# Routing of the first half of the tokens moved behind layer 2, two of its sums split, and a norm's bias kept with the rows

## The chip, the core and the metric

The kernel runs on one core of a Trainium2 chip. A core has a matrix engine (TensorE, PE in the profile), three engines for elementwise work (VectorE or DVE, ScalarE or ACT, GpSimd or POOL), a queue engine (SyncE, SP), an on-chip memory of 128 partitions, accumulators (PSUM) that the matrix engine writes, and 16 DMA engines. The metric is the time of one execution on the device in microseconds (us); lower is better.

## The reference

One layer of a graph network with a mixture of experts, on 1250 tokens of 768 numbers in float32:

```python
xn = layernorm(x)
x = x + gnn(xn, edges) + performer(xn)      # two attention layers over the graph, linear attention
x = x + experts(layernorm(x))

# gnn: layer 1 has 4 heads of 192, layer 2 has 2 heads of 96
out2 = gat(gat(layer_norm(xn), 4 heads), 2 heads)
gnn = concat([xn, out2]) @ Wu + bu

# experts: 8 experts, each token goes to its best 2
probs = softmax(flat @ router_w.T)
top, idx = top_k(probs, 2)
weights = top / balance[idx], normalised to sum 1  # balance: from the sum of probs over all tokens
h = silu(flat @ w1[e].T); y = h @ w2[e].T
out = sum over the token's two experts of weight * y
```

The edges are 20,000 drawn ones and a loop on every token.

## The kernel before

**Tiles.** The tokens are ten tiles of 125 rows. Tiles 0 to 4 are the first half, 5 to 9 the other half. The residual rows x live on chip in `acc[:, t, :]`; a row there is DX = 770 numbers wide: 768 values, and behind them two columns for the row's mean and the reciprocal of its deviation (rstd).

**Up to layer 2.** The program builds the adjacency counts, runs layer 1 and the performer attention, and puts the part of the sum that is known without layer 2 into `acc` (`updates`, line 886).

**Layer 2.** `second_layer(h, half)` (line 933) computes head h of layer 2 for one half of the destination tokens. It has ten steps, one for each tile of source tokens. A step (`attend`, lines 816 to 826) is a chain: ScalarE makes two exponentials (L816, L818, both named `e_b`), VectorE takes the larger of the two (L820), caps it at 1 and multiplies by the edge counts (L822, `p_b`), and five matmuls add that into five PSUM tiles (L826, `pa_b`). After ten steps the sums are divided by their denominators (L945, L946) into `o2s`, called `o_5` to `o_9` for the other half.

The first half's two heads run first. The other half's two heads follow, 20 steps in all, and the first half's further work is drawn in between them through the generator `first_half` (line 1180), one piece for each step until it is used up. That work is, for each tile:

- `out_turned` (L950): the layer-2 output is transposed (`tr_o`, L150) and copied by ScalarE (`oT`, L955)
- `updated` (L960): eight matmuls with the layer-2 rows of Wu (L966) give 768 sums in one PSUM tile of two banks, VectorE adds them to the row (L971), and takes the row's statistics (L129, L130)
- `stored` (L993), once for a half: rstd of its rows, mean and rstd put beside the rows (L997, L998), and the rows written to DRAM on SP's queue, for the first half to two places, `x2_d` and `xh_d`
- `update_turned` (L976): the row is transposed (`tr_xm`) and copied (`xT`, L980)
- `logits` (L985): six small matmuls with the router's weights

Then the routing of the first half, nearly all of it on VectorE and in one go: `placed(…, 0, …)` (line 1097) ranks the eight logits of each token (L1114 to L1119), counts each expert's tokens by two matmuls (`pcum`, L1122 and L1123) and prefix sums (L1085), and finds each choice's position; `rows_of(0)` (L1146) writes one-hot rows for those positions.

In these steps the order on each engine is chosen by a list scheduler from the program's order and dependences.

**From there on the order is written by hand** for TensorE, VectorE, ScalarE and GpSimd: each runs its instructions in the order of the program. A loop over `i` from 0 to 7 takes the other half's five tiles through the same stages, one stage later for each i: `out_turned` of tile 5+i, `update_turned` of tile 3+i, `updated` of tile 4+i, `logits` of tile 2+i. Within it, `first_tiles` (line 1152) builds for each of the eight experts the list of its first 125 tokens out of the first half: masks at i = 0, and at i = 1 ten matmuls (`plist`, L1173) and the indices (`take`, L1175). Right after it GpSimd starts eight gathers (L1218), one for each expert's first tile, out of `xh_d`. At its end come `normed` and `turned` for the first tiles.

**Experts.** An expert tile q is 125 gathered rows. `normed(q)` (L1224) normalises them: for q < 8 VectorE makes the bias, minus mean times rstd (`nb`, L1229), and ScalarE applies scale and bias (`xme`, L1230); for later tiles VectorE does it alone (L1232). Then the rows are transposed (`tr_xe`, L150; `xTe`, L1242), multiplied with w1 (`ph`, L1260), gated (`hw`, L1269 on ScalarE and L1270 on VectorE), transposed again (`tr_he`, `hT`) and multiplied with w2 (`po`, L1489). VectorE works on the other half's routing, and the lists of all later tiles, between the gates of the first eight tiles. The second weights (`ew2`, eight loads of 768 KB on SP) are loaded when the updates are done. Results go to DRAM, are gathered by halves (L1506), added (L1515) and stored (L1516).

Of the kernel before, what the change touches and what calls it, by code (L numbers as in the profile page):

```python
# [9 lines left out]
F32 = mybir.dt.float32  # L10
# [3 lines left out]
AF = mybir.ActivationFunctionType  # L14
ALU = mybir.AluOpType
# [4 lines left out]
D = 768  # L20
P = 125
NT = N // P
KD = D // 128
H1, C1 = 4, 192
H2, C2 = 2, 96
MH, HD, MF = 12, 64, 32
NE, FI = 8, 256


NQ = NE + (2 * (P * NT // 2 - P) + P * NT + NE * (P - 1)) // P  # L30
DX = D + 2
NQ1 = (2 * N + NE * P // 2) // P
BIG = 8192.0
assert NQ == 33
# [39 lines left out]
def kernel(  # L74
# [3 lines left out]
    nc = tc.nc  # L78
# [729 lines left out]
    TH_ = NT // 2  # L808
# [148 lines left out]
        transposed(psum, o2s[t], [(0, C2), (C2, C2)], keep_o2, f"o2{t}", bufs=bufs)  # L957
        oTs[t] = oT

    def updated(psum, t):  # L960

        oT = oTs.pop(t)
        po = psum.tile([P, 2, 512], F32, tag="po", name=f"po2_{t}", bufs=1)
        for hb in range(2):
            for j in range(H2):
                nc.tensor.matmul(  # L966
                    po[:, hb, :384], oT[:, j, :], wub[:, j, hb * 384 : (hb + 1) * 384],
                    start=(j == 0), stop=(j == H2 - 1),
                )
        xa = acc[:, t, :D].rearrange("p (a c) -> p a c", a=2)  # L970
        nc.vector.tensor_tensor(xa, po[:, :, :384], xa, ALU.add)  # L971
        stats_of(g2p, acc[:, t, :D], mv3[:, t, :], f"c{t}")

    x2Ts = {}
# [1 line left out]
    def update_turned(psum, t, bufs=None):  # L976
        xT = g2p.tile([128, KD, P], F32, tag="xT", name=f"xT_{t}", bufs=2)

        def keep_xm(b0, n, pt):
            nc.scalar.copy(xT[:, b0 : b0 + n, :], pt[:, :n, :])  # L980

        transposed(psum, acc[:, t, :D], BLOCKS, keep_xm, f"xm{t}", bufs=bufs)
        x2Ts[t] = xT

    def logits(pl, t):  # L985

        xT = x2Ts.pop(t)
        for k in range(KD):
            nc.tensor.matmul(pl, xT[:, k, :], rw[:, k, :], start=(k == 0), stop=(k == KD - 1))
# [3 lines left out]
    def stored(hf):  # L993

        t0, t1 = hf * TH_, (hf + 1) * TH_
        rs3 = rs3s[hf] = rstd_of(small, mv3, "c", t0, t1)
        nc.vector.tensor_copy(acc[:, t0:t1, D : D + 1], mv3[:, t0:t1, 0:1])  # L997
        nc.vector.tensor_copy(acc[:, t0:t1, D + 1 : DX], rs3.unsqueeze(2))  # L998
        for t in range(t0, t1):
            nc.sync.dma_start(out=x2_t[:, t, :], in_=acc[:, t, :DX])  # L1000
            if not hf:
                nc.sync.dma_start(out=xh_t[:, t, :], in_=acc[:, t, :DX])

# [92 lines left out]
    def placed(psum, hf, pl):  # L1096

        hs = slice(hf * TH_, (hf + 1) * TH_)
        three, big8 = [P, TH_, NE], [P, TH_, NE, NE]
        off = rtc.tile(three, F32, tag="off", name=f"off_{hf}")  # L1100
        nc.vector.tensor_tensor(
            off, mv3[:, hs, 0:1].to_broadcast(three), csum.unsqueeze(1).to_broadcast(three), ALU.mult
        )
        nc.vector.tensor_tensor(off, pl, off, ALU.subtract)
        nc.vector.tensor_tensor(lg[:, hs], off, rs3s[hf].unsqueeze(2).to_broadcast(three), ALU.mult)
        if hf:

            nc.vector.tensor_reduce(red[:, 0, :], lg, AX.X, ALU.max)
            nc.vector.tensor_tensor(prob, lg, red[:, 0, :].unsqueeze(2).to_broadcast([P, NT, NE]), ALU.subtract)
            nc.scalar.activation(prob, prob, AF.Exp)  # L1110
        cmp, eq = (big[:, 3010 + 320 * i : 3330 + 320 * i].rearrange("p (t a b) -> p t a b", t=TH_, a=NE) for i in range(2))
        others = lg[:, hs].unsqueeze(2).to_broadcast(big8)
        own = lg[:, hs].unsqueeze(3).to_broadcast(big8)
        nc.vector.tensor_tensor(eq, others, own, ALU.is_equal)  # L1114
        nc.vector.tensor_tensor(eq, eq, before.unsqueeze(1).to_broadcast(big8), ALU.mult)
        nc.vector.tensor_tensor(cmp, others, own, ALU.is_gt)
        nc.vector.tensor_tensor(cmp, cmp, eq, ALU.add)
        nc.vector.tensor_reduce(rank[:, hs], cmp, AX.X, ALU.add)
        nc.vector.tensor_scalar(sel[:, hs], rank[:, hs], 2.0, None, op0=ALU.is_lt)  # L1119
        yield  # L1120
        pcum = psum.tile([P, 2, TH_, NE], F32, tag="rt" if hf else "tr", name=f"pcum_{hf}", bufs=1)
        nc.tensor.matmul(pcum[:, 0], upper, sel[:, hs], start=True, stop=True)  # L1122
# [12 lines left out]
        picked(0, hs, pos[:, hs].unsqueeze(2).to_broadcast([P, TH_, 2, NE]), pick)  # L1135
        over2 = rtc.tile([P, TH_ * 2, NT - 1], F32, tag="over2", name=f"over2_{hf}")
        nc.vector.tensor_tensor(
            over2, at[:, 0, hs].rearrange("p t k -> p (t k)").unsqueeze(2).to_broadcast([P, TH_ * 2, NT - 1]),
            tens[:, 1:].unsqueeze(1).to_broadcast([P, TH_ * 2, NT - 1]), ALU.is_ge,
        )  # L1140
        nc.vector.tensor_reduce(nth[:, hs].rearrange("p t k -> p (t k)"), over2, AX.X, ALU.add)
        nc.vector.scalar_tensor_tensor(r_[:, hs], nth[:, hs], -float(P), at[:, 0, hs], op0=ALU.mult, op1=ALU.add)

    def rows_of(hf):
        hs = slice(hf * TH_, (hf + 1) * TH_)
        nc.vector.tensor_tensor(  # L1146
            oh_r[:, hf * NT : (hf + 1) * NT, :],
            r_[:, hs].rearrange("p t k -> p (t k)").unsqueeze(2).to_broadcast([P, NT, P]),
            col.unsqueeze(1).to_broadcast([P, NT, P]), ALU.is_equal,
        )  # L1150
# [28 lines left out]
    def first_half():  # L1179
        for t in range(TH_):  # L1180
            out_turned(ps_c, t)
            updated(ps_c, t)
            yield
        stored(0)
        for t in range(TH_):
            update_turned(ps_c, t)
            yield
            pl = ps_c.tile([P, NE], F32, tag="tr", name=f"plg_{t}")
            logits(pl, t)
            nc.scalar.copy(lraw[:, t, :], pl)  # L1190
        for _ in placed(ps_c, 0, lraw):
            pass
        rows_of(0)

    fh = first_half()
    for h in range(H2):
        for _ in second_layer(h, 1):
            next(fh, 0)
    for _ in fh:
        pass  # L1200
    closed(gap_, pa_, psc_)
# [22 lines left out]
    def normed(q):  # L1224
        xg = xgs[q]
        xm = exa.tile([P, D], F32, tag="xm", name=f"xme_{q}", bufs=1)
        if q < NE:
            nb = exa.tile([P, 1], F32, tag="nb", name=f"nb_{q}")
            nc.vector.scalar_tensor_tensor(nb, xg[:, D : D + 1], -1.0, xg[:, D + 1 : DX], op0=ALU.mult, op1=ALU.mult)  # L1229
            nc.scalar.activation(xm, xg[:, :D], AF.Identity, bias=nb, scale=xg[:, D + 1 : DX])  # L1230
        else:
            nc.vector.tensor_scalar(  # L1232
                xm, xg[:, :D], xg[:, D : D + 1], xg[:, D + 1 : DX], op0=ALU.subtract, op1=ALU.mult
            )
        xms[q] = xm

# [49 lines left out]
    manual_ = tc.manual_schedule(engines={ET.PE, ET.DVE, ET.Activation, ET.Pool})  # L1286
    manual_.__enter__()
    plg = ps_x.tile([P, TH_, NE], F32, tag="rt", name="plg")
    ft = first_tiles(ps_x)
    for i in range(TH_ + 3):  # L1290
        if i < TH_:
            out_turned(ps_x, TH_ + i, bufs=3)
        if i == 0:
            next(ft)
        if 2 <= i <= TH_ + 1:
            update_turned(ps_x, TH_ + i - 2, bufs=3)
        if i == TH_ + 1:
            stored(1)
        if 1 <= i <= TH_:
            updated(ps_x, TH_ + i - 1)  # L1300
        if i == 1:
            for _ in ft:
                pass
            for q in range(NE):
                gather(q)
        if i >= 3:
            logits(plg[:, i - 3, :], TH_ + i - 3)
        if i == TH_:
            normed(0)
# [212 lines left out]
    rt = routed()  # L1522
# [117 lines left out]
```

## Time and profile before

| | us |
|---|---|
| median of three runs | 1060.87 |
| lowest and highest | 1057.02, 1064.84 |
| the profiled execution | 1066.33 |
| its span in the profile | 1064.5 |
| TensorE busy | 972.1 |
| VectorE busy | 646.6 |
| ScalarE busy | 386.3 |
| GpSimd busy | 158.1 |

The profile is one execution on the chip. A row of the groups or of the timeline names the start or the busy time, the engine, the source line, the operation, the output and the inputs, the shape, and how many instructions it stands for; in brackets, how long the engine had been idle before and what released it. PEld is TensorE's weight load, which runs beside its matmuls. The granted clock is the share of full speed at which TensorE was allowed to run. "issue" is time in which the engine waited for nothing that the profile shows. Matmul ends are modelled, so a busy TensorE is not always one at its peak, and neighbouring rows can overlap slightly.

### The profile page before, as it was taken

What the parts mean: (1) busy time and instruction counts of PE and PEld (TensorE: products, weight loads), DVE (VectorE), ACT (ScalarE), POOL (GpSimd) and SP (SyncE); (2) the same over time, 40 slices, a digit from 0 to 9 for tenths busy, and PEclk for the clock granted to TensorE, in tenths of its full rate; (3) what the DMA queues carried; (4) which work ended last, traced back from release to release, by engine and by line L of the source; (5) the groups of instructions that cost most, each with busy time, mean ns of one, the idle gap of its engine ahead of it and who ended that gap; (6) DMA issues with size and microseconds to landing.
All of it is one profiled execution on the core that took longest, in us unless ns stands there. A gap on an engine that the chain in (4) does not pass through costs nothing. (4 is left out here: it accounts for less than half of the span.)

```text
span 1064.5 us, 12124 instructions
## 1 busy us (share of the span) xinstructions
PE 972.1 (91%) x4323; PEld 663.0 (62%) x4323; DVE 646.6 (61%) x1407; ACT 386.3 (36%) x662; POOL 158.1 (15%) x157
## 2 busy tenths in 40 slices
PE   6899999999979989999999899999998979987980
PEld 2775455546645557777776765566677667765750
DVE  7699556207457556667768849576587454453441
ACT  1653333310000075566555610065465254322320
POOL 1010000000000000000000202432100402275533
PEclk9999999999889999999999999999998889998995
DMA  8410000212321010000022422111163565455442
GB/s 209 138 40 24 15 22 13 104 74 77 117 91 59 15 57 17 24 24 23 2 83 115 133 69 99 64 45 53 59 203 113 132 215 177 134 174 152 127 124 85
DMA packets 55424, 93.19 MB, mean 88 GB/s; under 512 B 22704, under 2 KB 29040, under 8 KB 55354
## 3 DMA queue, kind: packets, MB, share of 16 engines
q1 hardware_dynamic: 30966, 73.63, 20.4%
q0 software_dynamic: 15904, 17.02, 5.9%
q10 hardware_dynamic: 8484, 1.65, 0.9%
q8 instruction: 39, 0.64, 0.3%
q14 instruction: 31, 0.25, 0.1%
HBM read 75.53 MB, written 27.04 MB: 96 GB/s over the span
## 5 line engine op out<-in xcount | busy, mean ns | idle before, releaser
L826 PE MATMUL pa_a<-acc,p_a 125*125 125x197 f32 x800 | 143.5, 335 | 5.8 <-DVE h L850 3.4
L826 PEld LDWEIGHTS pa_a<-acc,p_a 125*125 125x125 f32 x800 | 135.0, 189 | 22.0 <-issue 12.4
L695 PE MATMUL pg<-W,xnT 128*125 128x396 f32 x240 | 84.4, 516 | 6.2 <-DVE acc L698 6.2
L897 PE MATMUL po<-wu_sb,xnT 128*125 128x384 f32 x240 | 82.0, 490 | 5.1 <-ACT acc L901 3.9
L820 DVE SCALAR_TENSOR_TENSOR e_a<-e_a,e_a 125x625 f32<-125x625 f32 x80 | 67.2, 846 | 27.9 <-ACT e_a L816 14.3
L530 PE MATMUL pk_q<-xnT,wq_sb 128*128 128x375 f32 (+1 forms) x216 | 81.5, 516 | 2.5 <-PEq L744 1.7
L822 DVE SCALAR_TENSOR_TENSOR p_a<-e_a,cntT 125x625 f32<-125x625 f32 x80 | 64.4, 811 | 29.7 <-PE pa_a L826 27.2
L530 PE MATMUL pk_k<-xnT,wk_sb 128*128 128x375 f32 (+1 forms) x216 | 82.0, 515 | 0.0
L816 ACT ACTIVATE e_a<-rowt_a,s 125x625 f32<-125x625 f32 x80 | 64.7, 817 | 37.6 <-DVE p_a L822 34.0
L346 DVE TENSOR_SCALAR ohd<-iota,dst_f 125x125 bf16<-125x125 int16 (+1 forms) x170 | 51.6, 304 | 40.3 <-PE pe L353 40.3
L1489 PE MATMUL po<-ew,hT 128*125 (+1 forms) x192 | 70.6, 513 | 5.5 <-DVE hT L1280 5.0
L493 DVE CUSTOM_DVE_ANT_0 junk<-nmr,rows 125x1250 f32<-125x1250 bf16 x40 | 58.3, 1457 | 27.1 <-DMA rows<-sr_d 21.5
L695 PEld LDWEIGHTS pg<-W,xnT 128*125 128x125 f32 x240 | 46.9, 196 | 43.1 <-DVE acc L698 6.8
L818 ACT ACTIVATE e_a<-rowt_a,s1x 125x625 f32<-125x625 f32 x80 | 64.0, 814 | 21.5 <-DVE e_a L820 21.1
L1260 PE MATMUL ph<-ew,xTe 128*125 (+1 forms) x288 | 69.3, 392 | 0.0
L897 PEld LDWEIGHTS po<-wu_sb,xnT 128*125 128x125 f32 x240 | 43.6, 188 | 35.8 <-ACT acc L901 6.5
L1260 PEld LDWEIGHTS ph<-ew,xTe 128*125 128x125 f32 x288 | 55.6, 195 | 12.0
L530 PEld LDWEIGHTS pk_q<-xnT,wq_sb 128*128 128x128 f32 x216 | 39.8, 189 | 36.4 <-issue 17.2
L342 DVE TENSOR_SCALAR ohs<-iota,smod,wgt 125x313 bf16<-125x313 int16 x170 | 60.6, 356 | 0.0
L535 ACT ACTIVATE sT_q<-pk_q,kb 128x375 f32<-128x375 f32 (+1 forms) x18 | 10.8, 602 | 135.2 <-PE pk_q L530 135.2
L1489 PEld LDWEIGHTS po<-ew,hT 128*125 128x125 f32 x192 | 36.2, 196 | 29.4 <-issue 5.2
L826 PEld LDWEIGHTS pa_b<-h,p_b 125*125 125x125 f32 x400 | 49.0, 192 | 8.2 <-DVE p_b L822 2.3
(349 smaller groups left out, 1543.6 us busy)
## 6 DMA issues: line engine op xcount, KB each, us to landing
y_d<-y SPq DMA_DIRECT2D x23, 375.0 KB
ew<-in_w1T SPq DMA_DIRECT2D x8, 768.0 KB
ew<-in_w2T SPq DMA_DIRECT2D x8, 768.0 KB
nmr<-nm_d SPq DMA_DIRECT2D x20, 305.2 KB
rowt_a<-ab_d SPq DMA_DIRECT2D x8, 610.4 KB
x_d<-acc SPq DMA_DIRECT2D x10, 376.0 KB
acc<-in_x SPq DMA_DIRECT2D x10, 375.0 KB
xr<-in_x SPq DMA_DIRECT2D x10, 375.0 KB
```

The source lines that it names most:

```text
L342: nc.vector.tensor_scalar(oh_s[:, :TH], iota[:, :TH], smod[:, c : c + 1], wgt[:, c : c + 1], op0=ALU.is_equal, op1=ALU.mult)
L493: nc.vector.tensor_tensor_reduce(out=junk, in0=nm, in1=row, scale=1.0, scalar=-3.0e38, op0=ALU.add, op1=ALU.max, accum_out=mx_col)
L530: nc.tensor.matmul(pk[:, :w], w_sb[:, k, f * 128 : (f + 1) * 128], xnT[:, k, t0 * P : (t0 + n) * P], start=(k == 0), stop=(k == KD - 1),)
L695: nc.tensor.matmul(pg, xnT[:, k, t * P : (t + 1) * P], W12[:, k, cs], start=(k == 0), stop=(k == KD - 1))
L816: nc.scalar.activation(e1, rowt[:, 0, :], AF.Exp, bias=s[:, h, 0, u : u + 1])
L818: nc.scalar.activation(e2, rowt[:, 1, :], AF.Exp, bias=sx[:, h, u : u + 1])
L820: nc.vector.scalar_tensor_tensor(e1, e1, 1.0, e2, op0=ALU.min, op1=ALU.max)
L822: nc.vector.scalar_tensor_tensor(p, e1, 1.0, cntT[:, u, hf * HN : (hf + 1) * HN], op0=ALU.min, op1=ALU.mult)
L826: nc.tensor.matmul(pas[i][:, :cw], p[:, i * P : (i + 1) * P], hv, start=(u == 0), stop=(u == NT - 1))
L897: nc.tensor.matmul(po[:, hf, :384], xnT[:, k, ts], wu_sb[:, k, cs], start=(k == 0), stop=False)
L1260: nc.tensor.matmul(ph, xT[:, k, :], ew1[:, whose_r[q], k, :].rearrange("p o i -> p (o i)"), start=(k == 0), stop=(k == KD - 1),)
L1489: nc.tensor.matmul(po[:, hf, :384], hT[:, c, :], ew2[:, e_r, c, hf * 384 : (hf + 1) * 384].rearrange("p o n -> p (o n)"), start=(c == 0), ...
```

## The change

There are three edits.

**Where the first half's routing stands.** `first_half` now ends with the logits. Its pieces are no longer taken one a step from the first step on, but spread over the 20 steps of the two heads (at steps 1, 3, 4, 6, 8 and 9 of the first head, counted from 0, and 1, 3, 4, 6, 7 and 9 of the second; there are eleven pieces, so the last call finds nothing left), and a tile's logits are one piece behind its transposing. The ranks are placed in the hand-ordered loop at i = 0, the rest of `placed` at i = 1 after the update of tile 5, `rows_of` and the masks of `first_tiles` at i = 2 after the update of tile 6, and the lists with the eight gathers at i = 3 after the update of tile 7. `pcum_0` uses the three-slot PSUM tag "tr" of that loop.

**Sums in two places.** For i = 2 and 4, tiles 6 and 8, `updated` writes its two halves of 384 sums to two PSUM tiles of the tag "ph" in place of the single tile "po", and adds them with two VectorE instructions.

**Bias with the rows.** A row is one number longer. `stored` writes minus mean times rstd there, and `normed` for q < 8 has no VectorE instruction any more: ScalarE reads scale and bias from the gathered row.

```diff
-DX = D + 2
+DX = D + 3
...
-    def updated(psum, t):
+    def updated(psum, t, apart=False):
...
-        po = psum.tile([P, 2, 512], F32, tag="po", name=f"po2_{t}", bufs=1)
+        if apart:
+            pos = [psum.tile([P, 384], F32, tag="ph", name=f"po2_{t}_{hb}", bufs=2) for hb in range(2)]
+        else:
+            po = psum.tile([P, 2, 512], F32, tag="po", name=f"po2_{t}", bufs=1)
+            pos = [po[:, hb, :384] for hb in range(2)]
...
-        nc.vector.tensor_tensor(xa, po[:, :, :384], xa, ALU.add)
+        if apart:
+            for hb in range(2):
+                nc.vector.tensor_tensor(xa[:, hb], pos[hb], xa[:, hb], ALU.add)
+        else:
+            nc.vector.tensor_tensor(xa, po[:, :, :384], xa, ALU.add)
...
-        nc.vector.tensor_copy(acc[:, t0:t1, D + 1 : DX], rs3.unsqueeze(2))
+        nc.vector.tensor_copy(acc[:, t0:t1, D + 1 : D + 2], rs3.unsqueeze(2))
+        nc.vector.scalar_tensor_tensor(
+            acc[:, t0:t1, D + 2 : DX], mv3[:, t0:t1, 0:1], -1.0, rs3.unsqueeze(2), op0=ALU.mult, op1=ALU.mult
+        )
...
-        pcum = psum.tile([P, 2, TH_, NE], F32, tag="rt" if hf else "tr", name=f"pcum_{hf}", bufs=1)
+        pcum = psum.tile([P, 2, TH_, NE], F32, tag="rt" if hf else "tr", name=f"pcum_{hf}", bufs=1 if hf else 3)
...
         stored(0)
-        for t in range(TH_):
-            update_turned(ps_c, t)
+        for t in range(TH_ + 1):
+            if t < TH_:
+                update_turned(ps_c, t)
+            if t:
+                pl = ps_c.tile([P, NE], F32, tag="tr", name=f"plg_{t - 1}")
+                logits(pl, t - 1)
+                nc.scalar.copy(lraw[:, t - 1, :], pl)
             yield
-            pl = ps_c.tile([P, NE], F32, tag="tr", name=f"plg_{t}")
-            logits(pl, t)
-            nc.scalar.copy(lraw[:, t, :], pl)
-        for _ in placed(ps_c, 0, lraw):
-            pass
-        rows_of(0)
...
-        for _ in second_layer(h, 1):
-            next(fh, 0)
+        for u, _ in enumerate(second_layer(h, 1)):
+            i = h * NT + u
+            if i * 11 // 18 != (i + 1) * 11 // 18:
+                next(fh, 0)
...
-            nb = exa.tile([P, 1], F32, tag="nb", name=f"nb_{q}")
-            nc.vector.scalar_tensor_tensor(nb, xg[:, D : D + 1], -1.0, xg[:, D + 1 : DX], op0=ALU.mult, op1=ALU.mult)
-            nc.scalar.activation(xm, xg[:, :D], AF.Identity, bias=nb, scale=xg[:, D + 1 : DX])
+            nc.scalar.activation(xm, xg[:, :D], AF.Identity, bias=xg[:, D + 2 : DX], scale=xg[:, D + 1 : D + 2])
...
-    ft = first_tiles(ps_x)
+    fp, ft = placed(ps_x, 0, lraw), first_tiles(ps_x)
...
         if i == 0:
-            next(ft)
+            next(fp)
...
-            updated(ps_x, TH_ + i - 1)
+            updated(ps_x, TH_ + i - 1, apart=i % 2 == 0)
         if i == 1:
+            for _ in fp:
+                pass
+        if i == 2:
+            rows_of(0)
+            next(ft)
+        if i == 3:
             for _ in ft:
                 pass
             for q in range(NE):
```

More of the change, by code (lines that the diff above doesn't have):

```diff
@@ L966, in updated @@
                 nc.tensor.matmul(
-                    po[:, hb, :384], oT[:, j, :], wub[:, j, hb * 384 : (hb + 1) * 384],
-                    start=(j == 0), stop=(j == H2 - 1),
+                    pos[hb], oT[:, j, :], wub[:, j, hb * 384 : (hb + 1) * 384], start=(j == 0), stop=(j == H2 - 1)
                 )
         xa = acc[:, t, :D].rearrange("p (a c) -> p a c", a=2)
-        nc.vector.tensor_tensor(xa, po[:, :, :384], xa, ALU.add)
+        if apart:
[3 more added lines that the diff above has]
+            nc.vector.tensor_tensor(xa, po[:, :, :384], xa, ALU.add)
         stats_of(g2p, acc[:, t, :D], mv3[:, t, :], f"c{t}")
@@ L1227, in normed @@
         if q < NE:
-            nb = exa.tile([P, 1], F32, tag="nb", name=f"nb_{q}")
-            nc.vector.scalar_tensor_tensor(nb, xg[:, D : D + 1], -1.0, xg[:, D + 1 : DX], op0=ALU.mult, op1=ALU.mult)
-            nc.scalar.activation(xm, xg[:, :D], AF.Identity, bias=nb, scale=xg[:, D + 1 : DX])
+            nc.scalar.activation(xm, xg[:, :D], AF.Identity, bias=xg[:, D + 2 : DX], scale=xg[:, D + 1 : D + 2])
         else:
             nc.vector.tensor_scalar(
-                xm, xg[:, :D], xg[:, D : D + 1], xg[:, D + 1 : DX], op0=ALU.subtract, op1=ALU.mult
+                xm, xg[:, :D], xg[:, D : D + 1], xg[:, D + 1 : D + 2], op0=ALU.subtract, op1=ALU.mult
             )
```

## The prediction

> **What bounds the kernel now.** I read the page's totals first, then a table of stages around the code that changes, then the waits and the order of time in each.
>
> ```profile
> span 1064.5 us, 12124 instructions
> PE 972.1 (91%) x4323; PEld 663.0 (62%) x4323; DVE 646.6 (61%) x1407; ACT 386.3 (36%) x662; POOL 158.1 (15%) x157
> PEclk9999999999889999999999999999998889998995
> ```
>
> TensorE works 91% of the span. The third row has tenths of full clock: 8s in slices 30 to 32 (a slice is 26.6 us, so about 798 to 851). What the change can win is idle PE, or PE at a low clock, there. By stages (columns: window and length, busy time of PE, PEld, DVE, ACT, POOL, granted clock, DMA share, GB/s):
>
> ```profile
> 768.60:797.30 28.70, 28.14 (x176) 22.01 (x174) 25.46 (x51) 17.78 (x30) 1.34 (x1) 1.00 0.68 220
> 797.30:823.50 26.20, 21.71 (x166) 20.34 (x166) 19.55 (x53) 15.59 (x29) 0.00 (x0) 0.89 0.30 107
> 823.50:854.20 30.70, 28.95 (x139) 20.43 (x139) 15.22 (x39) 7.42 (x20) 12.20 (x15) 0.82 0.51 133
> 854.20:897.90 43.70, 37.09 (x209) 32.01 (x210) 23.40 (x104) 23.33 (x46) 4.88 (x4) 0.88 0.69 227
> 897.90:930.00 32.10, 31.69 (x147) 22.20 (x147) 13.02 (x30) 10.22 (x20) 9.17 (x7) 1.00 0.36 110
> ```
>
> Layer 2's last 20 steps are the first two rows and end at 819.25 with the last p_b; the other half's updates follow to 854, the first experts to 898. From 898 PE is full, and after it to 1036 it is 89% busy with 11.7 us idle: what is won before 898 should reach the end. The seam at 819 in order of time, PE's rows:
>
> ```profile
> 819.30 1.33 PE L826 MATMUL pa_b<-h,p_b 125*125 125x97 f32 x10 [1.90 <-DVE p_b L822]
> 820.81 0.41 PE L1122 MATMUL pcum<-sel,upper 125*125 125x40 f32 x2 [0.18 <-DVE sel L1119]
> ...
> 823.55 1.04 PE L150 MATMUL tr_o<-ident,o 125*96 125x125 f32 x4 [1.91 <-DVE first L1156]
> 824.68 5.48 PE L966 MATMUL po<-wub,oT 96*125 96x384 f32 x8
> ```
>
> PE waits twice for DVE, which has the first half's routing in its queue: the last p_b stands behind three rank operations (817.24 to 818.45), and tr_o behind pcum's reading, in whose PSUM slot it goes. Then L966's eight products take 5.48 us, against 2.75 in the update at 787: the clock was 0.51 from 821.3 to 834.9. In the experts' first stage the waits are
>
> ```profile
> ACT xme L1230 <- issue: 15.1, 5, 4.7
> PEld tr_xe L150 <- ACT xme L1230: 8.1, 6, 2.4
> PE tr_xe L150 <- ACT xme L1230: 7.0, 5, 2.2
> ```
>
> and xme is late for its bias, not for its gather. VectorE's two rows and ScalarE's next:
>
> ```profile
> 872.25 1.45 DVE L1146 TENSOR_TENSOR big<-r__19595,col 125x1250 bf16<-125x1250 f32 x1
> 873.63 0.15 DVE L1229 SCALAR_TENSOR_TENSOR nb<-acc 125x1 f32<-125x1 f32 x1
> 873.86 1.03 ACT L1230 ACTIVATE xme<-acc,nb 125x768 f32<-125x768 f32 x1 [3.21 <-issue]
> ```
>
> A bias of 0.15 us is queued behind a chunk of the second half's routing, ACT's xme starts 0.23 later, and PE's tr_xe follows. The same pair stands at 867.80/868.04, 878.13/878.36, 884.35/884.59 and 889.47/889.71.
>
> **The change, part by part.**
>
> Layer 2's steps (50.65 us to 819.25). The rank operations leave the stretch before the last p_b: it starts about 1.1 us earlier. The 11 pieces of side work are spread over 18 of the 20 steps rather than one on each of the first eleven: the five updates and the stores fall in the first head's ten steps, the five tr_xm (the first at its very end) and logits in the second's. First ten: DVE 20 x 0.81 for attention and 5 x 2.19 for the updates (0.96 add, 1.02 stats, 0.21) is 27.2 us, PE less (7 us of attention, 5 x 3.15). Second ten: PE 7 + 5 x 2.5 = 19.5, below the chain's own pace: L820 starts at 809.49, 811.92, 814.08, 816.51, so 2.3 us a step, 23. The sum of 50.2 is 0.5 less than now. Bounds: PE's idle time and its half-clock window at 800 could all go (3 + 1.7, less what DVE holds: +3), or the 1.05 us of ACT copies behind each logits stretch three or four chain-bound steps (-3). I take +0.5.
>
> The other half's updates (819.25 to the second expert tile's turning, tr_xe at 858.10: 38.85 us). tr_o no longer waits for pcum, and three slots replace one: 1.91 of idle goes. The ranks now follow the last p_b on DVE among the ten o_ operations, pcum comes after the first update's products, rows_of (1.46) after the stats of the second, the lists after the third's. I replayed the order on each engine with the durations above at full clock: tr_o at 1.6, pcum 5.3, tr_xm of tile 6 at 10.9 (it waits 1.45 for the add queued behind the routing), plist about 15.5, take 18.5 (now 13.5 after the last p_b), last add 24.9, tr_xe(1) at 32.6 to 34.1. That is 4.8 to 6.2 earlier; I take 5. Split sums: an add of 768 is 0.957, two of 384 by the stats row's half (0.55 for 384) about 1.1, so +0.16 twice, under DVE's 2.4 us idle in each update; without that cover 0.3 in all. One more scalar_tensor_tensor a half (0.17) and 4 of 3,080 bytes a row (0.13% of the row traffic): nothing, and if nothing hid them 0.5. On POOL the eight gathers (1.21 + 0.30 us each to issue) move with the lists, past nothing else there. The stores on SP's queue now start one to two steps later, so all ten end near 838, not 833.6; the gathers on POOL, which start 1.7 us after the stores' end now (835.29), start near 839.8 and the first lands 7 (as the lone gathers near 1044) to 12.6 later (gathers in traffic), 27.5 to 33 on this count: the replay's spread comes from it. ACT itself now waits for that landing, with xT of tile 9 and the table load queued behind it.
>
> Most of these 5 us are the clock. The Trainium skill (TensorE: Matmul & The Clock Gate, "HAM oscillation") warns of PE gaps over some 3.4 us; the gaps here are 1.90 and 1.91 and the clock was 0.51 for 13.6 us all the same, after windows in which PE was busy 75% and 59% (2.55 of 3.40, 1.82 of 3.10). By the rule the change would win the idle time alone, some 2; by the trace 11.6 us of half-speed work shrink by up to 5.8, of which new waits take part. The trace decides: 5, with 2 as the low end.
>
> The first experts (858 to 898). Eight nb operations (1.2 us of DVE, unimportant) go, and with them ACT's wait behind the routing chunks. PE's idle before tr_xe is 7.0 us, and 1.7 more lies in the half-clock window at 876. Replayed, ph(6) comes 7.6 us earlier. Next in line is DVE: gate hw L1270 of tile q+1 stands behind the chunk after hw of q, but DVE idles 1.7 to 2.7 before each, so a tile can gain no more than that, five times: 9.6. Against that the two gathers of the second pass then land inside the expert weights' traffic (870 to 884, 353 GB/s); they took 9.6 and 12.6 us from start to use, and may take 0.5 to 5 back. I take 4.5, bounds 0 and 7.6.
>
> Sum: 0.5 + 5 + 4.5 = 10.0. The profiled execution took 1066.33 (span 1064.5), so 1056.3; the three timed runs lie lower, median 1060.87, and the same 10 us makes 1050.9: 1051.
>
> **The rivals.**
>
> More than that (0.17): PE's half-clock stretches at 855.8 and 876 go too, being fed without gaps. 5.92 + 3.40 busy us halve: 4.7 more, of which a part is counted; 15 in all, 1046. For it: both follow gaps. Against: the table loads before the first gates remain.
>
> Half of it is lost (0.25): either the clock stays at half for two or three windows after 819 (1.7 each), because PE still waits for o_5 behind the ranks, or the hand-outs downstream set the pace: from 1036 to 1064 PE works 0.39 us, and the end is gathers of 7 us and stores. For it: POOL waits 28.4 us for L1515 there. Against: PE is 98.7% busy to 930. 5 us: 1056. That the change doesn't do what it says belongs here: if the landing of the gather, not nb, holds xme, the 4.5 is nothing.
>
> Slower (0.18): the gathers. They start 4.5 us later while the experts' second weights (eight loads of 768 KB, today from 857.28, just behind the gathers' end at 855.2) follow the last update and start up to 5 earlier: the last four gathers meet them. The gathers alone ran at 173 GB/s, 2.2 us each. The Trainium skill (DMA: Bandwidth & Descriptors, "Queues, rings and completion order") says that an engine takes turns between queues by whole packets; an even split makes 4.4 each, within the 5 us that a tile takes, and is hidden; the two gathers in traffic came 4.5 apart. Should the loads get three quarters, it is 8.7 each, ACT stands still 3.7 on each of four and everything behind it too: 14.8, minus the 10 gained, 1066. It decides from 7.5 us between landings.
>
> Forecast 0.40: 1046 to 1056.
>
> **How the numbers follow.** A measurement of this kernel can tell about 1%: 1050.3 and 1071.5. Faster: half of the forecast, the whole of the first rival, a little of the second: 0.40. Slower: half of the last rival and the steps' bad end on top of it: 0.14. Same: 0.46. The range takes the better case's middle and the slower one's: 1043 to 1066.
>
> **What would show it.** Right: no idle over 1 us before tr_o after layer 2, L966 x8 near 2.8 there, clock over 0.9 from 823 to 854; no DVE work between a landed gather and its xme, tr_xe's wait under 3 us in all. Wrong: ACT's xme waiting for DMA by several us, pa_b steps over 2.6 us apart in the second head, or a PE stretch of 0.5 in new places.

## The result, and the profile after

The changed kernel takes 1073.78 us (median of four runs, 1071.39 to 1076.05) against 1058.96 for the kernel before: a ratio of 1.011, 95% interval 1.0074 to 1.0146. A second set of nine runs gave 1.0097 (1.0069 to 1.0125). By these ratios it is slower by 10 to 12 us, by the medians of the two sets by 13 to 15, where 10 us less had been forecast. Single runs of one kernel lie up to 14 us apart (71 runs of the kernel before: 1052 to 1067), so the sizes below rest on such ratios, each against runs of the kernel before on the same chip. They are not the plain quotients of the medians, and they have a noise of their own: twelve more runs of the kernel before, against itself, gave 1.0029 (0.9998 to 1.0061). The profiles are single executions, and are read stage by stage, each from its own start.

Totals of the changed kernel's page:

```profile
span 1074.2 us, 12126 instructions
PE 975.2 (91%) x4323; PEld 666.3 (62%) x4323; DVE 644.2 (60%) x1403; ACT 386.0 (36%) x662; POOL 160.4 (15%) x157
PEclk9999999999689999999999999999996797999995
```

The work is the same; from slice 31 on (counted from 1; a slice is 26.9 us, so from 806) the clock row now has 6, 7, 9, 7 where it had 8, 8, 8, 9. The stages that matter, for each kernel from its own start, beginning with the last product of layer 2's first half (columns: window and length, busy time of PE, PEld, DVE, ACT, POOL, granted clock, DMA share, GB/s). The rows are: the other half's first head, up to the reading of its first sum (L945); from there to the end of layer 2, called the second head; the updates up to the turning of the second expert tile; the experts' first tiles up to ph of the seventh; and from there to the first second product (L1489 before, L1506 after). TensorE's program has the ninth tile's turning ahead of ph of the eighth, so a wait for the ninth tile stands in the last row. Before:

```profile
767.20:795.50 28.30, 28.08 (x178) 22.12 (x177) 24.81 (x49) 16.80 (x30) 1.81 (x1) 1.00 0.70 224
795.50:820.70 25.20, 22.34 (x176) 20.92 (x174) 18.92 (x43) 17.37 (x30) 0.00 (x0) 0.93 0.28 98
820.70:858.10 37.40, 32.80 (x161) 24.02 (x161) 18.98 (x66) 11.23 (x26) 12.20 (x15) 0.78 0.45 121
858.10:891.50 33.40, 27.67 (x151) 23.41 (x152) 18.02 (x76) 17.31 (x34) 4.88 (x4) 0.89 0.79 264
891.50:898.20 6.70, 6.70 (x45) 5.96 (x44) 4.25 (x20) 2.21 (x6) 0.00 (x0) 1.00 0.53 148
```

After:

```profile
773.60:798.10 24.50, 23.66 (x151) 18.96 (x150) 22.38 (x42) 16.07 (x27) 1.81 (x1) 1.00 0.81 258
798.10:833.00 34.90, 32.21 (x201) 29.82 (x199) 20.59 (x50) 18.44 (x33) 0.00 (x0) 0.76 0.24 86
833.00:868.40 35.40, 30.48 (x160) 21.63 (x160) 20.02 (x63) 11.34 (x26) 11.84 (x10) 0.85 0.31 94
868.40:892.50 24.10, 23.56 (x151) 20.82 (x152) 18.16 (x77) 16.56 (x33) 0.33 (x7) 1.00 0.80 254
892.50:912.90 20.40, 9.18 (x44) 7.92 (x43) 4.36 (x20) 2.44 (x7) 4.92 (x4) 0.67 0.71 213
```

The first head gains 3.8 us, the second loses 9.7, at a mean clock of 0.76 (with the border at the first head's last matmul, 2.2 and 8.2). The updates gain 2.0, the first expert tiles 9.3, and 13.7 are lost at once before the ninth tile. The sum is 139.3 us against 131.0, 8.3 longer. The other differences of the two spans are not put down to the change: TensorE's instructions, in the same order, had come 6.4 us later to the start of these rows (slice 11 of the clock row has 6 where it had 8), and the rest after them took 5.1 less, where two profiles of the kernel before differ by 7.5. (A second profile of the kernel before has 132.2 for the sum, a second one of the changed kernel 138.9.)

Two places make the loss. In the second head, PE's rows of the changed kernel in order of time:

```profile
807.18 1.31 PE L826 MATMUL pa_b<-h,p_b 125*125 125x97 f32 x10
808.32 0.59 PE L150 MATMUL tr_xm<-ident,acc 125*128 125x125 f32 x4
809.63 0.68 PE L150 MATMUL tr_xm<-ident,acc 125*128 125x125 f32 x2 [0.72 <-ACT xT L987]
810.11 2.26 PE L826 MATMUL pa_b<-h,p_b 125*125 125x97 f32 x10
812.16 2.58 PE L996 MATMUL plg<-rw,xT 128*125 128x8 f32 x12
```

Ten attention matmuls take 1.31 us and then 2.26, twelve of the logits 2.58 (1.47 at 805.85): from 809.2 TensorE runs at half clock, after idle gaps of under 0.8 us only: in the three stretches of 3.4 us ahead of it PE was busy 3.21, 2.53 and 3.07 us.

And before the ninth tile (q = 8), in order of time, VectorE's list, GpSimd's gather, VectorE's norm and PE's turning:

```profile
885.25 0.17 DVE L1377 TENSOR_TENSOR take<-list_i 125x16 int32<-125x16 f32 x1
893.12 1.29 POOL L1230 DMA_INDIRECT acc<-x_d,take  x1 [24.39 <-PE tr_xe L150]
905.85 0.68 DVE L1242 TENSOR_SCALAR xme<-acc 125x768 f32<-125x768 f32 x1 [11.37 <-DMA acc<-x_d,take]
906.68 1.49 PE L150 MATMUL tr_xe<-ident,xme 125*128 125x125 f32 x6 [11.22 <-DVE xme L1242]
```

The list was there at 885.4; the gather started 7.7 us later and its rows arrived 12.7 us after that. It reads `x2_d`, and so waits until the other half's five row stores have landed. (The row names a PE operation, but that had ended at 892.65 and the gather depends on none so late; a run below shows what released it.) Before the change the gather started at 883.36, one us after its list, and the first products had nothing to wait for.

### The profile page after: what moved, and what is told of

Same layout as the page of the kernel before. It is cut to its first block, busy times and chain, and to the rows that moved or that the text cites. A ratio compares the mean times of both kernels' runs of the same rounds, so it can differ in the third digit from the quotient of the medians.

```text
span 1074.2 us, 12126 instructions
## 1 busy us (share of the span) xinstructions
PE 975.2 (91%) x4323; PEld 666.3 (62%) x4323; DVE 644.2 (60%) x1403; ACT 386.0 (36%) x662; POOL 160.4 (15%) x157
## 4 chain that ended last, share of the span: by engine, by line
PE 67%; DVE 12%; DMA 8%; issue 6%; ACT 4%; POOL 3%; POOLq 0%; SPq 0%; DVEq 0%; ACTq 0%
PE pa_a L826 12%; PE pk_q L530 6%; PE pg L695 6%; PE po L897 6%; PE pk_k L530 5%; PE pa_b L826 4%; PE po L1506 3%; PE po L899 3%; PE ph L1270 3%; PE po L970 2%; DMA rows<-sr_d 2%; PE pe L353 2%; DVE junk L493 2%; DVE ohd L346 2%; DMA nmr<-nm_d 1%
## 5 line engine op out<-in xcount | busy, mean ns | idle before, releaser
L826 PEld LDWEIGHTS pa_a<-acc,p_a 125*125 125x125 f32 x800 | 135.0, 189 | 21.7 <-issue 12.1
L1506 PE MATMUL po<-ew,hT 128*125 (+1 forms) x192 | 68.7, 502 | 5.5 <-DVE hT L1290 5.0
L818 ACT ACTIVATE e_a<-rowt_a,s1x 125x625 f32<-125x625 f32 x80 | 64.1, 814 | 21.5 <-DVE e_a L820 21.1
L826 PEld LDWEIGHTS pa_b<-h,p_b 125*125 125x125 f32 x400 | 52.6, 205 | 6.8 <-DVE p_b L822 1.8
L826 PE MATMUL pa_b<-h,p_b 125*125 125x97 f32 x400 | 54.0, 288 | 1.4 <-DVE p_b L822 1.3
```

The costliest lines, as they stand in the source:

```text
L818: nc.scalar.activation(e2, rowt[:, 1, :], AF.Exp, bias=sx[:, h, u : u + 1])
L826: nc.tensor.matmul(pas[i][:, :cw], p[:, i * P : (i + 1) * P], hv, start=(u == 0), stop=(u == NT - 1))
L1506: nc.tensor.matmul(po[:, hf, :384], hT[:, c, :], ew2[:, e_r, c, hf * 384 : (hf + 1) * 384].rearrange("p o n -> p (o n)"), start=(c == 0), ...
```

## The experiments

The theory after the result: (a) spreading the pieces puts the transposes in the second head, where the clock falls; (b) the bias in the rows does make the first tiles fast, but the ninth stands behind DMA, so nothing of it is kept; (c) the moved routing starts the gathers later and so pushes the stores behind them. The rivals are named in each expectation. (Where an expectation gives the second head 24 or 30 to 33 us, it counts from the last o_ operation of the first head, some 3 us after the start of the rows above.)

**The bias alone.** The kernel before with `DX = D + 3`, the stored column and the `normed` of the change.

> The kernel before with one edit: the bias of the norm stored with the rows, no nb operation. Theory (the second pass's gathers are the bound of the experts' start): ph(7) comes about 8 to 12 us earlier after tr_xe(1) than in the kernel before, and then PE waits 8 to 12 us at tr_xe of tile 8 for its gather, because the gather waits for the other half's rows to land in DRAM; the time stays within 3 us of the kernel before. Rival (the forecast: the idle time before tr_xe is a gain): 4 to 8 us less than before, and tr_xe of tile 8 waits under 3 us.

Measured: ratio 1.0001 (0.9979 to 1.0022), 20 runs. (Where this expectation says ph(7), the last of the fast tiles is ph(6): the ninth tile's turning stands ahead of ph(7).) From tr_xe(1) to ph(6) it took 26.4 us in place of 33.4; then the ninth tile:

```profile
876.15 1.22 POOL L1221 DMA_INDIRECT acc<-x_d,take  x1 [25.21 <-DVE prob L1456]
890.24 0.68 DVE L1233 TENSOR_SCALAR xme<-acc 125x768 f32<-125x768 f32 x1 [7.05 <-DMA acc<-x_d,take]
```

ph(6) starts at 881.19, the ninth tile's turning waits 6.9 us, and the first second product comes 15.6 us after ph(6), where it took 6.7 before. The forecast's 7.6 us up to ph(6) are there, 7.0 of them, and the next wait takes them back whole. The gather starts 2 us after its list and then takes 14.1 us, so here, other than expected, the wait is mostly for the transfer and little for the rows' stores.

**The spreading alone.** The kernel before with

```diff
-        for _ in second_layer(h, 1):
-            next(fh, 0)
+        for u, _ in enumerate(second_layer(h, 1)):
+            i = h * NT + u
+            if i * 11 // 18 != (i + 1) * 11 // 18:
+                next(fh, 0)
```

> The kernel before with one edit: the eleven pieces of the first half's work spread over the 20 steps by the rule of the changed kernel, routing still at the end of them. Theory (transposes and logits in the second head's steps hold up the chain of the attention steps): layer 2's last matmul comes 5 to 8 us later, with granted clock near 0.5 in a stretch of the second head; time 5 to 8 us over the kernel before. Rival (only where the pieces stand changed, the sum of the work is the same): within 2 us.

Measured: ratio 1.0044 (1.0019 to 1.0068), 4.7 us. Layer 2's last matmul comes 61.0 us after the start of the stages, against 53.4, with the clock at half from 805 to 825. The theory's first expectation holds, and the time falls just short of its 5 to 8 us.

**Everything but the spreading.** The changed kernel with those lines put back.

> The changed kernel with the spreading undone: one piece in each of the first eleven steps; routing moved and bias in the rows as there. Theory: layer 2's 20 steps take 50 us again in place of 56, and the time falls 5 to 8 us below the changed kernel, to 1064 to 1069 if the rest costs what the trace shows at the second pass's first gather. Rival (the moved routing or the gathers cost the time): stays within 2 us of the changed kernel.

Measured: ratio 1.0052 (1.003 to 1.0075). The 20 steps take 52.9 us again. What remains, 5.5 us, is more than the bias alone (0) and, next, the move alone.

**The move alone.** That kernel without the bias in the rows.

> The kernel before with the routing moved into the other half's updates and the sums of tiles 6 and 8 in two places; one piece a step in layer 2 as before, and nb still made by VectorE. Theory (the move alone is harmless: it delays the gathers by some 6.5 us against layer 2's end, and that costs only where the experts' first tiles are fast enough to wait for what is stored behind the gathers): the second expert tile's turning comes 2 to 4 us earlier after layer 2's end than before, ph(0) to ph(7) takes about 36 us as before, tile 8 waits under 2 us; time 0 to 4 us below the kernel before. Rival (the moved routing costs the 5 us by which the changed kernel without the spreading is slower): 4 to 7 us above.

Measured: ratio 0.9995 (0.9975 to 1.0016). By itself the move costs nothing, and by itself the bias gains nothing, but together they cost 5.5. The trace of the two together suggests how: the first gather starts 21.5 us after layer 2's last matmul, against 14.7 before, so the eight gathers are still in flight when the other half's rows are stored. In the kernel with everything but the spreading, the second pass's first gather starts 8 us after its list (872.56),

```profile
880.52 1.22 POOL L1228 DMA_INDIRECT acc<-x_d,take  x1 [24.57 <-DMA ew<-in_w2T]
```

and among its waits from 854 to 900 (in total, times, longest) are those for this gather's data, used at 891.86:

```profile
DVE xme L1240 <- DMA acc<-x_d,take: 10.1, 1, 10.1
PE tr_xe L150 <- DVE xme L1240: 9.9, 1, 9.9
```

With nb in VectorE's queue the ninth tile is not wanted before that. The three intervals together leave 2 to 10 us for this interaction, and some of it lies behind the ninth tile, where the profile's single run cannot settle it.

The move alone gave more than was asked. Its matmuls come in the same order, from the first to the last, as those of the kernel with everything but the spreading. Yet the second head took 31.8 us in its profile and 25.7 in the other's. First the move alone, then everything but the spreading:

```profile
798.60:830.40 31.80, 31.04 (x186) 30.16 (x185) 18.93 (x43) 16.86 (x29) 0.00 (x0) 0.66 0.29 103
```

```profile
794.40:820.10 25.70, 22.88 (x186) 21.43 (x184) 18.93 (x44) 16.41 (x29) 0.00 (x0) 0.95 0.28 97
```

VectorE's busy time is the same, and so are the 186 matmuls. TensorE's clock, 0.66 against 0.95, is the difference: 6 us that come or not from one execution to the next. All profiles without added matmuls, read from the first head's last matmul to the end of layer 2, say what the spreading adds to that. In the ten of kernels that take one piece a step, half clock lasted 1.9 to 6.8 us in seven and 16.6 to 21.6 in three, and the second head took 23.9 to 31.0 us. In five with the pieces spread it lasted 16.8 to 20.5 us in every one, and the head took 32.3 to 35.4. The long half-clock stretch is now and then there without the spreading; with it, it was there each time. And gaps alone do not bring it on. In the profile of the move alone the clock fell at 822.5, after 3.4 us in which TensorE's rows follow each other without a gap:

```profile
819.30 1.40 PE L996 MATMUL plg<-rw,xT 128*125 128x8 f32 x12
820.56 1.09 PE L826 MATMUL pa_b<-h,p_b 125*125 125x97 f32 x8
821.49 1.66 PE L996 MATMUL plg<-rw,xT 128*125 128x8 f32 x12
823.01 7.40 PE L826 MATMUL pa_b<-h,p_b 125*125 125x97 f32 x32
```

**The stores on more DMA engines.** The changed kernel with each row store in two.

```diff
-            nc.sync.dma_start(out=x2_t[:, t, :], in_=acc[:, t, :DX])
+            for rs_ in (slice(0, 120), slice(120, P)):
+                nc.sync.dma_start(out=x2_t[rs_, t, :], in_=acc[rs_, t, :DX])
```

(and likewise for `xh_t`).

> The changed kernel with one edit: each row store of 125 rows is two, of 120 and of 5 rows, so that more DMA engines share it. Theory (the gather of tile 8 waits for the other half's stores to land, which takes some 24 us): the stores land in under 12 us, POOL's first x_d gather starts within 2 us of its list, tr_xe of tile 8 waits under 4 us in place of 11, and the time falls 6 to 10 us. Rival (that gather waits for its own transfer beside the second weights): the wait stays over 8 us and the time within 2 us.

Measured: ratio 1.0053 (1.0029 to 1.0077) against 1.011 and 1.0097, so some 5 us come back, though the intervals just overlap. Its trace has the gather at 880.81, 1.0 us after its list (879.77), and the ninth tile waits 5.0. This settles what the gather had waited for: the row stores. The first half's stores of 125 rows, alone on the DMA engines, run in the kernel before at 123 GB/s and a DMA share of 0.32 (as much as five of 16); in pieces of 120 and 5 rows they ran here at 281 and 0.91 (802 to 815).

**The same stores on the kernel with the bias alone.**

> The kernel before with the bias in the rows, and each row store as two of 120 and 5 rows. Theory (behind the faster first tiles stands the gather of tile 8, which waits for the stores and then for the second weights' traffic): the gather starts within 1 us of its list, tile 8's turning waits 4 to 7 us in place of 10, time 3 to 7 us below the kernel before. Rival (the gain is lost elsewhere too): within 2 us of it.

Measured: ratio 0.9994 (0.997 to 1.0018). A miss: the gather starts with its list, at 877.44, but takes 14.8 us to arrive; the ninth tile waits 6.5. The second weights' loads, issued from 867 on, are the suspect, and the run with these loads behind the gathers, below, bears it out.

**Rows stored as they are made.** The bias alone, with each row stored after its update and only the three columns of statistics later.

> The kernel before with the bias in the rows, and each row of x stored as soon as it is updated, only the three columns of its statistics after them. Theory: the stores and the second weights' loads are done earlier by some 10 us, so the gather of tile 8 starts with its list and meets no traffic; its turning waits under 3 us, and the 10 us that the first eight tiles gain stay: 1047 to 1053. Rival (the 12-byte pieces of the statistics, or POOL's wait for more stores, take as long as the rows): the first gathers start later than 16 us after layer 2's end, or tile 8 still waits over 6 us; within 3 us of the kernel before.

Measured: ratio 0.998 (0.9956 to 1.0003). The wait falls to 3.7 us, about as hoped, but the gain of 8 does not come: in its profile the updates ran 5 us longer than with the bias alone (38.2 us to tr_xe(1), against 33.2), with the clock at half for 17.1 us after layer 2's end where the other had it back after 8.4.

**The second weights behind the gathers.** The bias alone, and

```diff
-    for e_ in range(NE):
-        nc.sync.dma_start(out=ew2[:, e_], in_=w2T[e_].rearrange("(c p) n -> p c n", p=128))
+    nc.sync.dma_start(out=ew2[:, 0], in_=w2T[0].rearrange("(c p) n -> p c n", p=128))
...
             gather(got)
             got += 1
+            if got == NE + 2:
+                for e_ in range(1, NE):
+                    nc.gpsimd.dma_start(out=ew2[:, e_], in_=w2T[e_].rearrange("(c p) n -> p c n", p=128))
```

> The kernel before with the bias in the rows, and seven of the eight loads of the second weights issued by GpSimd just behind the gathers of tiles 8 and 9 in place of SyncE's queue behind the rows' stores. Theory (after the stores it is this traffic that makes the gather of tile 8 take 12 to 15 us): that gather lands within 9 us of its start, tile 8 waits under 3 us, and the weights come in time for the second products; 5 to 9 us below the kernel before. Rival (the gather is slow by itself, or the weights now come late): tile 8 or a second product waits over 5 us, time within 3 us of the kernel before.

Measured: ratio 0.9978 (0.9952 to 1.0004). The gather of tile 8 arrives in 6.7 us and the tile does not wait at all. But the third gather now stands behind the loads in GpSimd's queue, and its tile waits:

```profile
915.24 1.51 PE L150 MATMUL tr_xe<-ident,xme 125*128 125x125 f32 x6 [5.39 <-DVE xme L1233]
```

The same edit on everything but the spreading:

> The changed kernel without the spreading, and with the loads of the second weights behind the gathers of tiles 8 and 9. Theory: with the traffic away the moved routing costs no more than the gathers' later start leaves of the stores' landing: 0 to 6 us below the kernel before. Rival (the moved routing costs 5 us for a reason other than the transfers at tile 8): 3 to 7 us above it.

Measured: ratio 1.0012 (0.9989 to 1.0035), so some 4 us of its 5.5 were that traffic. Its gather of tile 8 still starts 9.5 us after its list, and then arrives in 6.6; the tile waits 7.1.

**Copies on VectorE.** The changed kernel with the first half's transposed rows copied by VectorE in place of ScalarE.

> The changed kernel with one edit: the copies of the first half's transposed rows out of PSUM, in the second head's steps, are made by VectorE and not by ScalarE. Theory (the transposes placed in the second head wait for ScalarE's copies among the steps' exponentials, the gaps close the clock, and at half clock the steps are bound by TensorE): the second head takes 24 to 27 us in place of 30 to 33, under 5 us of it at half clock, and the time falls by 4 to 7 us below the changed kernel. Rival (VectorE is as late as ScalarE, or the clock closes for another reason): the second head stays at 29 us or more, the time within 2 us.

Measured: ratio 1.015 (1.01 to 1.02). A miss: the second head takes 38 us on the count of the rows above, with half clock from 810 to 824 and again from 828. ScalarE's copies alone are not what makes the second head slow. What else does stays open.

**TensorE kept busy.** The changed kernel with matmuls that wait for nothing, into PSUM columns that are not read, before steps 1 to 7 of the second head:

```diff
+            if h and hf and 0 < u < 8:
+                for i in range(2):
+                    nc.tensor.matmul(pas[i][:, 128:253], ident[:P, :P], ident[:P, :P], start=False, stop=False)
```

> The changed kernel with fourteen more matmuls of the identity (125 x 125, about 0.27 us each, 3.8 us in all, into PSUM columns that nothing reads) in steps 1 to 7 of the second head, two a step, which wait for nothing. Theory (gaps close the clock, and the half clock makes the steps long): under 5 us at half clock in the second head, which takes 24 to 28 us in place of 30 to 33, and the time falls 2 to 6 us below the changed kernel in spite of the added work. Rival (the steps' chain is long by itself): the second head takes as long or up to 4 us longer, and the time rises by 0 to 4.

Measured: ratio 1.0057 (1.0032 to 1.0082), against 1.0097 and 1.011 for the changed kernel: 4 to 6 us less, with intervals that overlap slightly, in spite of 3.8 us of work added. The first and second head:

```profile
769.60:794.00 24.40, 23.55 (x150) 18.89 (x150) 22.31 (x41) 16.01 (x27) 1.81 (x1) 1.00 0.82 260
794.00:822.80 28.80, 27.24 (x230) 25.38 (x228) 19.35 (x45) 18.28 (x33) 0.00 (x0) 1.00 0.22 78
```

The clock stays at 1.00 and the second head takes 28.8 us, not 34.9. The steps' chain could go this fast all along; the low clock made the head long, not the other way round. (The ninth tile then waits 12.1 us.) The same matmuls on the kernel before:

> The kernel before with the same fourteen matmuls. Theory: no half clock in the second head in its profile; the time within 2 us of the kernel before, its runs closer together. Rival (the chain sets the pace): 1 to 4 us more than before.

Measured: ratio 0.9989 (0.9967 to 1.0011). Nothing is gained or lost there beyond some 4 us. Its profile, of its slowest run, has no half clock in the second head, which takes 23.9 us from the first head's last matmul; in the kernel before the half clock lasted 3.4 us there in both profiles, and the head 24.1 and 24.6, so there was little to win.

**A version that beats both.** The bias alone with the seven loads behind all four gathers (`NE + 4` in the edit above):

> The kernel before with the bias in the rows, and seven of the eight loads of the second weights issued by GpSimd behind the gathers of tiles 8 to 11. Theory: no expert tile waits over 2 us for a gather up to 930 us, and 4 to 9 us below the kernel before. Rival (the weights now come late, or later tiles give it back): a second product waits over 4 us for its weights, or the end comes within 3 us of the kernel before.

Measured: ratio 0.9916 (0.9891 to 0.9941), median 1053.97. Here the bias's gain is kept in good part: from tr_xe(1) to the first second product it takes 36.6 us, against 40.1 before and 42.0 with the bias alone. The updates are 4.7 us shorter than before too, with half clock for 6.8 us of them and not 16.6, and the profile's one execution can't say whether that is more than chance. The ninth tile waits 2.4 us, and its gather and the loads behind the four are, in GpSimd's rows,

```profile
880.46 1.22 POOL L1221 DMA_INDIRECT acc<-x_d,take  x1 [25.75 <-DVE red L1459]
...
886.24 4.56 POOL L1560 DMA_DIRECT2D ew<-in_w2T  x6
```

With the fourteen matmuls as well:

> The last two edits together on the kernel before. Theory: 5 to 11 us below it. Rival: within 3 us of it.

Measured: ratio 0.9879 (0.9832 to 0.9926) in four runs, and once more, with

> The kernel before with the bias in the rows, the loads behind the four gathers and the fourteen matmuls, once more. 7 to 12 us below the kernel before.

0.988 (0.9833 to 0.9926) in six. By these ratios it is 1.2% below the kernel before, by the medians 1.1 and 0.8%. The intervals with and without the matmuls overlap, so their own share isn't settled. In both profiles the clock had fallen in the second head before the first of the added matmuls, and stayed at half for 6.8 us; after it came back it held until the last microsecond of the head.

**The change with both repairs**, and the changed kernel once more:

> The changed kernel with both repairs: the fourteen matmuls that wait for nothing in the second head, and seven loads of the second weights behind the gathers of tiles 8 to 11. Theory (the clock and the transfers at tile 8 are all of the loss): 4 to 10 us below the kernel before, within 4 us of the next kernel. Rival (the moved routing has a cost of its own, as by the rows' stores that meet the later gathers): between 2 us below and 4 us above the kernel before, with tile 8 waiting over 4 us still.

> The changed kernel, unchanged, for more of its runs beside the others and a second profile. 10 to 14 us over the kernel before; the second head's ten steps take 30 us or more with 8 us or more of it at half clock; the gather of tile 8 starts some 25 us after the rows' stores are issued and tile 8 waits 8 us or more.

Measured: 0.9987 (0.9967 to 1.0008) with the repairs, over 22 runs, and 1.0097 without. With the two causes gone the loss against the kernel before is gone, but the rival keeps a share: some 11 us by the ratios, 7 by the medians, still lie between this and the kernel with the bias and the same repairs. Its trace shows one place. The list is written at 880.25 and the gather starts at 888.57, 8.3 us later (3.5 and 3.8 in the other's two profiles); the ninth tile waits 5.4 (0.7 and 1.1). By the reading above, the moved routing's own gathers are late and meet the rows' stores, for which this gather waits; no run took this apart here. How much of the 11 us that is, and how much lies in what follows, stays open.

## Why the prediction was wrong

**Layer 2's steps, "I take +0.5", bounds -3 and +3.** This step failed first. The first head gained 3.8, more than was counted; the second lost 9.7. The sum took the second head at "the chain's own pace", 23 us, with TensorE "below" it at 19.5. TensorE's 19.5 was counted at full clock. At half clock it is the bound: with the clock kept up by added matmuls the head took 28.8 us in place of 34.9. The bound -3 was for copies in the chain; no bound was set for more half clock, though the profile had shown a stretch of it at 800. What closes the clock stays open (below). Worth -5.9 in the profile and -4.7 timed alone.

**The updates, +5.** Measured 2.0 (2 to 3 between the second profiles). Of the two gaps at the seam the one before the last p_b's matmuls went. The one before tr_o stayed: it waits 2.02 us for the ranks' sel in place of 1.91 for the lists. The clock was not kept: it fell at 826.2, in the second head already, and was back at 839.9, 7 us after the end of layer 2 in place of 14; over the stage it was 0.85 in place of 0.78, where over 0.9 had been named. Here the rule of the Trainium skill (TensorE: Matmul & The Clock Gate, "HAM oscillation") had given 2, and the trace, as it was read, 5. That is no merit of the rule: in the second head the clock fell after gaps of under 1 us, where the page speaks of some 3.4, and in the profile of the move alone it fell at 822.5 after 3.4 us in which PE's rows have no gap at all. What was wrong was to suppose that removing the gaps behind 819 would keep the clock up.

**The first experts, +4.5, bounds 0 and 7.6.** The replay's 7.6 us up to ph(6) were there: 9.3 with the change (6.7 between the second profiles), 7.0 with the bias alone. The price of the second pass's gathers, "0.5 to 5", was 13.7 (10.9 between the second profiles): one was sized by the latency seen before, when nobody waited for those gathers, and their start, which waits for stored(1), was not followed. The step's mechanism was named, but this cost was two to three times its upper end, so the sum of the step is -4.4 in place of +4.5.

**"From 898 PE is full ... what is won before 898 should reach the end."** It failed in a way that the row for 898 could not show: the stage was full because the transfers for it had come just in time (tile 8's gather started at 883.36, VectorE used its rows at 892.97, and TensorE turned them at 894.29). A faster stage ahead of it arrives before its data.

**Costed at nothing.** The split sums and the third column show in no run: the move alone, with the split sums, is 0.9995, and the bias alone, with the column, 1.0001, each good to some 2 us.

**Signs and readings.** Of the signs named for being wrong two came: steps of the second head over 2.6 us apart (its matmuls start at 810.11 and at 815.94), and half clock in new places. ScalarE's xme did not wait for DMA; VectorE's did, at the ninth tile. One reading was off: the three 8s of the clock row (slices 30 to 32, counted from 0) reach to 878, not to 851. No sum rests on it.

**The rivals.** The slower one had the right collision, gathers against the second weights, but at the last four of the first eight tiles, which waited for no DMA (ph(6) at 892.5). It ended at 1066, the range with it, and the median is 1073.8. The forecast gave slower by over 1% a chance of 0.14.

## What to carry to other kernels

When a wait is removed, follow the next consumer back to its data: list, store, gather, and what shares the DMA engines with each; idle time before it is not a gain until its own data can come that much earlier. Where half-clock stretches stand in a profile, a stage's TensorE time is a range of one to two; spreading the pieces over such a stage cost 4.7 us here, with nothing added to the work. Two edits that are each worth nothing can cost when both are in: test them apart and together.

## What was not expected of the hardware

Half clock came after idle gaps of under 0.8 us, with PE busy 74 to 94% of the three 3.4 us stretches before, and in the profile of the move alone after 3.4 us without a gap in PE's rows. So gaps alone don't account for it, and what closes the clock was not found. Fourteen matmuls that wait for nothing, 3.8 us in all, kept it at 1.00 through the second head of the changed kernel; in two other profiles it had fallen before the first of them. The same order of instructions took 52.9 or 59.0 us for 20 steps, with the clock as the only difference seen. The first half's stores of 125 rows moved 123 GB/s, and 281 once each was cut to 120 and 5. A gather of 125 rows was used 6.7 us after its start with the loads out of the way, and 11 to 15 beside them where its tile waited for it.
